# A four-layer cross-attention network on one core: where 1/sqrt is taken, which buffers a weight rounding uses, the rank of the first scans, and the place of some loads

## The chip, the cores and the metric

The kernel runs on one core of a Trainium2 chip. A core has a matrix engine (TensorE, PE in the profile; its weight loads are shown apart as PEld), VectorE (DVE), ScalarE (ACT), GpSimd (POOL), and SyncE (SP), whose only work here is to start transfers. The engines run side by side, each takes its own instructions strictly in order, and they wait for one another through semaphores. The metric is the device time of one execution in microseconds.

## What is computed

The input x has 4 batches of 512 rows and 512 columns (f32), and each batch has a context of 512 rows and 256 columns. Four layers follow; each adds a gated cross-attention part and then a gated feed-forward part (FFN) to x:

```python
x = x + tanh(g_xattn[0]) * mamba(ctx, layernorm(x))            # layer 0
x = x + tanh(g_ffn[0])   * ffn_2of4_sparse(layernorm(x))
x = x + tanh(g_xattn[1]) * attention(layernorm(x), ctx)        # layer 1
x = x + tanh(g_ffn[1])   * ffn_ternary(layernorm(x))
x = x + tanh(g_xattn[2]) * mamba(ctx, layernorm(x))            # layer 2
x = x + tanh(g_ffn[2])   * ffn_fp8_weights(layernorm(x))
x = x + tanh(g_xattn[3]) * attention_16_heads_qk_rmsnorm(layernorm(x), ctx)   # layer 3
x = x + tanh(g_ffn[3])   * ffn_1bit_weights_8bit_activations(layernorm(x))
```

The mamba parts are state-space scans: for each of 512 channels and 16 states, `state = state * exp(dt * A) + dt * u * B`, step by step over the 512 positions, and `y = sum over states of C * state`. What the scan needs (dt, u, B, C) comes from the context alone, so a scan can run well before its layer. Each layer norm, and each RMS norm of the queries and keys of layer 3, takes 1/sqrt of one number a row. In layer 2 the weights are first rounded to fp8 (e4m3) values. In layer 3's FFN activations are rounded to 8 bits a row, and the normalised hidden rows are scaled by gamma and shifted by beta.

## The kernel before

**Blocks.** x of a batch lies in four tiles of 128 x 512. `f01` (L1251) does layers 0 and 1 of a batch, `f23` (L1265) layers 2 and 3 up to the attention. They come in the order f01(0), f01(1), f23(0), f01(2), f23(1), f01(3), f23(2), f23(3), by the list `heads` (L1275). The next block's layer norm and mamba part is started inside the last matmuls of the current one (`nxt.start`, `nxt.turn`). A prologue (L1276) does the scan of layer 0, batch 0 alone. Layer 3's FFN, `l3f` (L1095), runs beside the blocks for batches 0 to 2 and alone for batch 3, as the tail (L1313).

**Side work.** Three lists of Python generators hold work to be put between the steps of the blocks: `side` (the scans, then the rounding of layer 3's weights to one bit, then `l3f`), `pres` (what comes before a scan: convolution, x_proj matmul, dt), and `prep` (the rounding of layer 2's weights to fp8, 36 half tiles). `tick(w)` (L139) gives each list credit in proportion to its rate and lets it issue steps until the credit is spent. A scan may not start before its own `pres` item is done (`waits()`). `finish(key)` issues the rest of an item at once where a block needs it. `phase[0]` is the place in `heads`, 0 to 5; 0 is f01(0).

**Order.** The lines are only recorded. A scheduler then puts each engine's instructions in order by a priority, which is the place of recording plus an offset: an instruction of lower number goes first among those that are ready. In `tick` the offset `BEHIND` is added for `prep`, and for `side` except in phase 0. The order is fixed when the kernel is built. Tiles of one tag in a pool share a fixed number of buffers, and an instruction that needs a buffer waits for those that still use it. All loads and stores named here but those of `keep` and of the scans' B and C ahead are started by SP, in order, so one that waits holds back those behind it.

**Scans.** `state` (L578) does one of 64 steps (16 states x 4 channel tiles): ACT exp into a PSUM bank `mb` (L581), POOL du x B into one of three buffers `db` (L582), DVE scan (L583), DVE times C (L584); then POOL adds into y (L602). Before it, `mamba_pre` (L472) works in four buffers of tag `mt`: it stores each u to DRAM and loads it again for the x_proj matmul (L508), one u before each of the four matmuls.

**First use of weights.** `unit` (L259) loads a raw f32 tile into one of four buffers `wr` (L264), ACT takes the high part (L256), POOL or DVE in turn the low part (L257), and the pair is stored to DRAM for later use. Later uses load the pair. This happens in f01(0) and at the start of others' first use.

**fp8 rounding.** `to_fp8` (L284) takes two buffers `wr`: one for the raw weights, one for `m`, the power of two of each element. DVE makes `m` (L290), ACT scales (L293), DVE adds and subtracts (L294, L295), and the result is stored to DRAM, from where `unit8` (L311) loads it in layer 2's FFN.

**1/sqrt.** `rsqrt` (L332) is one POOL operation, a power of -1/2 (L333), in place. `ln_stats` (L354) calls it for 1, 3 or 4 numbers a row, `kv` (L895) for 16, `q_pair` (L954) for 8, and `l3f` (L1175) for 1. DVE makes the numbers before (L363, L894, L953, L1174) and reads the result (L365, L1177), or ACT does (L899).

**Layer 3's FFN beside the blocks.** A token tile (`token`, L1129) loads x (`xl`, two buffers, L1135) and uses b1, gamma, beta and b2 spread over 128 rows (`rep`, five buffers, L1115), each loaded where it is needed. Two tokens run interleaved, the second half of one beside the first half of the next. The tail has buffers of its own, and pool `l3f` stays open while it runs.

Of the kernel before, what the change touches and what calls it, by code (L numbers as in the profile page):

```python
# [10 lines left out]
F32 = mybir.dt.float32  # L11
# [12 lines left out]
NT = S // 128  # L24
# [25 lines left out]
RATES = [0.75, 0.75, 0.75, 0.75, 0.75, 0.75, 0.75, 0.75]  # L50
RATE_FP8 = 0.15
RATE_PRE = 0.25


BEHIND = 1000
# [17 lines left out]
def tile_flamingo(ctx: ExitStack, tc: tile.TileContext, I, out):  # L73
# [65 lines left out]
    def tick(w):  # L139

        waits = lambda: side and any(k == (*side[0][0], "pre") for k, _ in pres)
        for q, r, i in ((pres, 1.0 if waits() else RATE_PRE, 0), (prep, RATE_FP8, 2), (side, rate[0], 1)):
            credit[i] += w * r
            behind = BEHIND if q is prep or q is side and phase[0] else 0
            while q and credit[i] > 0 and not (q is side and waits()):
                tc.cur_priority += behind
                try:
                    credit[i] -= next(q[0][1])
                except StopIteration:
                    q.pop(0)  # L150
                tc.cur_priority -= behind
            if not q:
                credit[i] = 0.0
# [130 lines left out]
    def to_fp8(dst, src):  # L284


        raw = T(wrp, [128, 512], F32, "wr")
        sy.dma_start(raw, src)
        m = T(wrp, [128, 512], F32, "wr")
        v.tensor_scalar(  # L290
            m.bitcast(I32), raw.bitcast(I32), 0x7F800000, 0x00400000, op0=ALU.bitwise_and, op1=ALU.bitwise_or
        )
        s.activation(raw, raw, AF.Copy, scale=2.0**-20)  # L293
        v.scalar_tensor_tensor(raw, m, 1.5 * 2.0**-6, raw, op0=ALU.max, op1=ADD)  # L294
        v.scalar_tensor_tensor(raw, m, 1.5 * 2.0**-6, raw, op0=ALU.max, op1=SUB)  # L295
        copy(dst, raw)
# [32 lines left out]
        return t  # L329


    def rsqrt(a, n):  # L332
        g.tensor_tensor(a, a, mhalf[:, :n], op=ALU.pow)  # L333

    def mm3(ps, lh, ll, rh, rl, start, stop):
        pe.matmul(ps, lh, rh, start=start, stop=False)  # L336
# [17 lines left out]
    def ln_stats(xs, small=small):  # L354
        n = len(xs)
        st = small(6 * n)
        mv = small(2 * n)
        for t in range(n):
            v.bn_stats(st[:, 6 * t : 6 * t + 6], xs[t])
# [3 lines left out]
        v.tensor_scalar(rs[:, :n], mv2[:, :, 1], EPS, None, op0=ADD)  # L363
        rsqrt(rs[:, :n], n)
        v.scalar_tensor_tensor(rs[:, n:], mv2[:, :, 0], -1.0, rs[:, :n], op0=MUL, op1=MUL)  # L365
        return rs, mv

# [104 lines left out]
    def mamba_pre(l, b, mp, pp=None):  # L472
# [24 lines left out]
            yield 2.6  # L497
        xw = M("mt")
        sy.dma_start(xw[:, :320], I[f"M{l}_xp"][0])
        xd = mbps("xd")  # L500
        for d in range(4):
            if pp:
                u = ud[d]
            else:
                u = M("mt")
                copy(u, ud[d])
            c = slice(d * 80, d * 80 + 80)
            pe.matmul(xd[:80], xw[:, c], u, start=d == 0, stop=d == 3)  # L508

        xf = M("mt")  # L510
        s.copy(xf[:80], xd[:80])
# [362 lines left out]
    def kv(b, fp):  # L874

        cu = [unit("ctxT", 2 * b + k, p=fp, tag="fc") for k in range(2)]
        for qd in range(4):
# [17 lines left out]
            rsqrt(ss[:, 16:], 16)  # L895
# [25 lines left out]
    def l3x(b, xs, xT, nxt):  # L921
        with tc.tile_pool(name=nm("r3"), bufs=2) as rp:
# [8 lines left out]
            def q_pair(p):  # L931
# [22 lines left out]
                rsqrt(ss[:, 8:], 8)  # L954
                for j in range(2):
                    qs[2 * p + j] = qn, ss[:, 8 + 4 * j : 12 + 4 * j]

# [136 lines left out]

    def l3f(b, lp, ws, ps_of=mbps, tail=None):  # L1095

        nbuf = {"rep": 5, "Y": 2, "q16": 2, "qT": 1, "yT": 4, "sq": 1, "xl": 2}
        if tail:
            nbuf = {"rep": 1, "Y": 4, "q16": 4, "qT": 2, "yT": 8, "sq": 1}

# [6 lines left out]
        kept = {}  # L1107

        def rep(n, f):

            if (n, f) in kept:
                return kept[n, f]
            tag = f"rep{n}{f}" if tail else "rep"
            r = lp.tile([128, 512], F32, tag=tag, name=nm("rep"), bufs=nbuf["rep"])
            sy.dma_start(r, I["L3_" + n][512 * f : 512 * f + 512].partition_broadcast(128))  # L1115
            if tail:
                kept[n, f] = r
            return r

        def turned(x, tag):  # L1120

# [7 lines left out]
        def token(t):  # L1129

            if tail:
                x = tail[t]
            else:
                x = L("xl", [128, 512], F32)
                sy.dma_start(x, xsc[b * NT + t])  # L1135
            rs, _ = ln_stats([x], smallL)
            yield 0.7, 1.6
            y = L("Y", [128, 2048], F32)
            z = y[:, 0:512]
            s.activation(z, x, AF.Identity, scale=rs[:, 0:1], bias=rs[:, 1:2])  # L1140
# [11 lines left out]
            for f in range(4):  # L1152
                c = slice(f * 512, f * 512 + 512)
                b1r = rep("b1", f)
                ps = ps_of("l1")
                for k in range(4):
                    pe.matmul(ps, xq[:, k * 128 : k * 128 + 128], ws["w1", k][:, f], start=k == 0, stop=k == 3)  # L1157
                v.scalar_tensor_tensor(y[:, c], ps, sc[:, 1:2], b1r, op0=MUL, op1=ADD)  # L1158
# [16 lines left out]
            rsqrt(m2[:, 3:4], 1)  # L1175
# [42 lines left out]
        gens = [token(t) for t in range(NT)]  # L1218
        if not tail:

            old = iter(())
# [78 lines left out]
    mctx.close()  # L1300
    with tc.tile_pool(name="l3f", bufs=2) as lp:
        ws3 = l3f_weights(lp)
        for b in range(2):
            side.append(((b,), l3f(b, lp, ws3)))
        rate[0] = RATES[6]
        f23(heads[6], heads[7])
        finish((1,))
        side.append(((2,), l3f(2, lp, ws3)))
        rate[0] = RATES[7]
        f23(heads[7], None)  # L1310
        finish((2,))
# [89 lines left out]
```

## Time and profile before

| | |
|---|---|
| median of three runs | 3705.31 us (3698.0 to 3706.08) |
| the profiled execution | 3685.68 us, of which the trace spans 3683.9 us |
| mean granted clock of TensorE in it | 0.928 of full speed |
| end of the prologue, by the last update of x there (L649) | 188 us |
| end of f01(0), f01(1) | 718 us, 1135 us |
| end of f23(0), f01(2), f23(1) | 1569 us, 1972 us, 2399 us |
| end of f01(3), f23(2), f23(3) | 2734 us, 3158 us, 3584 us |

The ends of blocks are taken from DVE's updates of x (L430, L437), rounded to whole microseconds. Work of neighbouring blocks overlaps at these borders. A line such as `L365 DVE SCALAR_TENSOR_TENSOR sm<-sm,sm 128x3 ... x20 | 9.6, 482 | 20.0 <-POOL sm L333 20.0` is read so: source line, engine, operation, what it writes and reads, how often, total busy time in us, mean of one in ns, idle time of the engine just before them in us, and what ended most of that idle time. In a list of waits the numbers are the total, how many, and the longest. Granted clock is a share of TensorE's full speed.

### The profile page before, as it was taken

Reading aid. Unit: us, or ns where it says so; the run is one execution under the profiler, and the core shown is the slowest. Engines: PE = TensorE matmul, PEld = TensorE weight load, DVE = VectorE, ACT = ScalarE, POOL = GpSimd, SP = SyncE. Lnnn points to the kernel's source line nnn. Section 1 sums busy time; section 2 is a strip of 40 time slices with the busy share of each in tenths; the row PEclk is TensorE's granted clock in tenths of the full one; section 3 lists DMA queues with packets and bytes.
Section 4 is the critical chain, followed back from the end, with each engine's and each line's share of the span. In section 5 each row is a group of like instructions: output and inputs, shape, how many; then the busy total and the mean of one; then the engine's idle time right before and its main releaser. Section 6 shows DMA issues by size and latency. Waiting matters only on the chain. (4 is left out here: it accounts for less than half of the span.)

```text
span 3683.9 us, 40258 instructions
## 1 busy us (share of the span) xinstructions
PE 3112.8 (84%) x12216; PEld 1979.4 (54%) x12216; DVE 2541.4 (69%) x4162; ACT 1983.4 (54%) x4405; POOL 1722.2 (47%) x1351
## 2 busy tenths in 40 slices
PE   7785875889778788899888778899999998898985
PEld 3364444565556545475565545475767554564542
DVE  7957856789688787887678878855334455454437
ACT  6455355354545667544544656543435666366644
POOL 5515856637556785744665778700101122222112
PEclk9997887999899899999999899999999999999997
DMA  8577567876876564385676543287664343554310
GB/s 272 186 264 255 182 197 257 287 250 210 272 246 208 189 187 135 108 292 189 211 243 216 169 157 106 90 296 261 227 209 163 120 135 95 166 172 122 110 42 31
DMA packets 310232, 693.10 MB, mean 188 GB/s; under 512 B 31712, under 2 KB 33120, under 8 KB 310016
## 3 DMA queue, kind: packets, MB, share of 16 engines
q1 hardware_dynamic: 256176, 589.86, 47.3%
q10 hardware_dynamic: 53840, 100.68, 9.2%
q8 instruction: 97, 1.59, 0.2%
q14 instruction: 119, 0.97, 0.1%
HBM read 525.46 MB, written 164.95 MB: 187 GB/s over the span
## 5 line engine op out<-in xcount | busy, mean ns | idle before, releaser
L581 ACT ACTIVATE mb<-dt,nA 128x512 f32<-128x512 f32 x512 | 347.1, 689 | 398.2 <-DVE db12x L584 52.0
L333 POOL TENSOR_TENSOR sm<-sm,mhalf 128x8 f32<-128x8 f32 (+4 forms) x96 | 138.8, 1446 | 483.2 <-DVE sm L363 174.1
L678 PE MATMUL gate<-xT,w 128*128 128x512 f32 x624 | 266.9, 428 | 75.4 <-ACT w L256 40.1
L985 PE MATMUL po<-pt,v 128*128 128x512 f32 x512 | 277.9, 631 | 28.3 <-ACT pt L824 22.3
L807 PE MATMUL S<-k,q 128*128 128x512 f32 x512 | 264.9, 620 | 22.2 <-ACT P L814 19.8
L814 ACT ACTIVATE P<-S,st,sm 128x512 f32<-128x512 f32 x256 | 199.9, 783 | 119.1 <-DVE st L812 117.5
L679 PE MATMUL gate<-xT,w 128*128 128x512 f32 x624 | 258.7, 415 | 1.4 <-DVE xT L257 1.4
L402 PE MATMUL acc<-w,hf 128*128 128x512 f32 x512 | 233.0, 614 | 25.6 <-DVE hf L705 14.3
L678 PE MATMUL up<-xT,w 128*128 128x512 f32 x624 | 246.7, 395 | 4.1 <-ACT w L256 4.0
L679 PE MATMUL up<-xT,w 128*128 128x512 f32 x624 | 245.6, 394 | 0.0
L808 DVE TENSOR_REDUCE st<-S 128x1 f32<-128x512 f32 x256 | 173.2, 684 | 92.9 <-PE S L807 91.2
L1003 PE MATMUL down<-wo,h 128*128 128x512 f32 x512 | 231.9, 603 | 0.7 <-DVE x L430 0.7
L333 POOL TENSOR_TENSOR sml<-sml,mhalf 128x1 f32<-128x1 f32 x32 | 18.5, 578 | 440.9 <-DVE sml L1174 229.9
L822 PE MATMUL pT<-ident,P 128*128 128x128 f32 x1024 | 168.7, 285 | 52.0 <-ACT P L814 27.3
L822 PEld LDWEIGHTS pT<-ident,P 128*128 128x128 f32 x1024 | 127.6, 146 | 136.3 <-ACT P L814 45.8
L681 PE MATMUL gate<-xT,w 128*128 128x512 f32 x432 | 181.3, 420 | 14.0 <-POOL w L257 13.8
L678 PEld LDWEIGHTS gate<-xT,w 128*128 128x128 f32 x624 | 125.0, 200 | 116.0 <-ACT w L256 41.8
L402 PEld LDWEIGHTS acc<-w,hf 128*128 128x128 f32 x512 | 99.0, 196 | 155.6 <-issue 113.3
L681 PE MATMUL up<-xT,w 128*128 128x512 f32 x432 | 169.2, 392 | 3.2 <-DVE w L257 3.2
L824 ACT COPY pt<-pT 128x512 f32<-128x512 f32 x256 | 145.9, 589 | 47.7 <-PE pT L822 46.5
L402 PE MATMUL acc<-w,h 128*128 128x512 f32 x352 | 159.7, 606 | 6.3 <-ACT fv L907 4.9
L336 PE MATMUL Q<-w,xT 128*128 128x256 f32 x512 | 156.7, 306 | 3.3 <-ACT xT L256 3.2
(288 smaller groups left out, 8971.9 us busy)
## 6 DMA issues: line engine op xcount, KB each, us to landing
bc<-dbc ACTq DMA_DIRECT2D x105, 512.0 KB, 5.7
w<-dL_g SPq DMA_DIRECT2D x81, 512.0 KB, 5.3
w<-dL_u SPq DMA_DIRECT2D x81, 512.0 KB, 4.6
w<-in_L_d_dram SPq DMA_DIRECT2D x68, 512.0 KB, 5.5
w<-dL_gu SPq DMA_DIRECT2D x48, 512.0 KB, 4.6
w<-dL_q SPq DMA_DIRECT2D x48, 512.0 KB, 5.1
rep<-in_L_b_dram SPq DMA_DIRECT2D x65, 256.0 KB, 3.9
dv<-fv ACTq DMA_DIRECT2D x64, 256.0 KB, 4.0
```

The costliest lines, as they stand in the source:

```text
L333: g.tensor_tensor(a, a, mhalf[:, :n], op=ALU.pow)
L402: pe.matmul(ps, h[:, c], w, start=first, stop=last)
L581: s.activation(ps, dt, AF.Exp, scale=nA[l][:, d * 16 + n : d * 16 + n + 1])
L678: pe.matmul(ps, wh[:, c], xT[k][:, 0], start=k == 0, stop=False)
L679: pe.matmul(ps, wh[:, c], xT[k][:, 1], start=False, stop=wl is None and k == 3)
L681: pe.matmul(ps, wl[:, c], xT[k][:, 0], start=False, stop=k == 3)
L807: pe.matmul(ps, q[:, c], k, start=True, stop=True)
L808: v.tensor_reduce(st[:, t : t + 1], ps, AX.X, ALU.max, negate=True)
L814: s.activation(p, ps, AF.Exp, scale=r, bias=m, accum_out=st[:, 8 + t : 9 + t])
L822: pe.transpose(ps[:, t * 128 : t * 128 + 128], pt[t][:, kt * 128 : kt * 128 + 128], ident)
L985: pe.matmul(po, vs[kt][:, c], u, start=kt == 0, stop=kt == 3)
L1003: pe.matmul(ps, hs[j][:, c], ws[j // 2][:, j % 2], start=j == 0, stop=j == 3)
```

## The change

- `tick` gives `side` no credit while it waits for its `pres` item, and ranks `side` behind in phase 0 too.
- `to_fp8` takes its two buffers from the tag `mt` (four, shared with `mamba_pre` and the dt weights), not from `wr`.
- `rsqrt` is done on DVE in phases 0 to 4 and the prologue, by 11 small operations: a first guess from the bits, -a/2, and three of Newton's steps of three operations each. From phase 5 on (set to 6 for the last two blocks) it stays on POOL. 62 of 128 calls move.
- `mamba_pre` loads three of the four u tiles before the first x_proj matmul, and the fourth before the last, with pauses between.
- `l3f` loads x one token ahead (three buffers `xl`) and the `rep` tiles one step ahead (seven buffers). The tokens' tiles lie in a pool of their own that is closed before the tail's pool is opened.

```diff
         for q, r, i in ((pres, 1.0 if waits() else RATE_PRE, 0), (prep, RATE_FP8, 2), (side, rate[0], 1)):
+            if q is side and waits():
+                continue
             credit[i] += w * r
-            behind = BEHIND if q is prep or q is side and phase[0] else 0
+            behind = BEHIND if q is not pres else 0
...
     def to_fp8(dst, src):
-        raw = T(wrp, [128, 512], F32, "wr")
+        raw = T(mp, [128, 512], F32, "mt")
         sy.dma_start(raw, src)
-        m = T(wrp, [128, 512], F32, "wr")
+        m = T(mp, [128, 512], F32, "mt")
...
-    def rsqrt(a, n):
-        g.tensor_tensor(a, a, mhalf[:, :n], op=ALU.pow)
+    def rsqrt(a, n, h=None, small=small):
+        if phase[0] >= SCANS:
+            g.tensor_tensor(a, a, mhalf[:, :n], op=ALU.pow)
+            return
+        w = small(2 * n if h is not None else 3 * n)
+        y, t = w[:, :n], w[:, n : 2 * n]
+        h = w[:, 2 * n :] if h is None else h
+        v.tensor_scalar(y.bitcast(I32), a.bitcast(I32), -0.5, float(0x5F3759DF), op0=MUL, op1=ADD)
+        v.tensor_scalar(h, a, -0.5, None, op0=MUL)
+        for i in range(3):
+            v.tensor_tensor(t, y, h, op=MUL)
+            v.tensor_tensor(t, t, y, op=MUL)
+            v.scalar_tensor_tensor(a if i == 2 else y, t, 1.5, y, op0=ADD, op1=MUL)
...
         sy.dma_start(xw[:, :320], I[f"M{l}_xp"][0])
+        if not pp:
+            for d in range(3):
+                u = M("mt")
+                copy(u, ud[d])
+                ud.append(u)
+            yield 2.6
         xd = mbps("xd")
         for d in range(4):
-            if pp:
-                u = ud[d]
-            else:
+            if not pp and d == 3:
                 u = M("mt")
                 copy(u, ud[d])
+                ud.append(u)
+                yield 1.3
...
-        nbuf = {"rep": 5, "Y": 2, "q16": 2, "qT": 1, "yT": 4, "sq": 1, "xl": 2}
+        nbuf = {"rep": 7, "Y": 2, "q16": 2, "qT": 1, "yT": 4, "sq": 1, "xl": 3}
...
+        def fetch(*vs):
+            if not tail:
+                for n, f in vs:
+                    ahead[n, f] = rep(n, f)
+
+        def fetch_x(t):
+            xls[t] = L("xl", [128, 512], F32)
+            sy.dma_start(xls[t], xsc[b * NT + t])
...
             rs, _ = ln_stats([x], smallL)
             yield 0.7, 1.6
+            fetch(("b1", 0))
...
+                if f < 3:
+                    fetch(("b1", f + 1))
...
+            if not tail and t + 1 < NT:
+                fetch_x(t + 1)
+            fetch(("gamma", 0), ("beta", 0))
             yield HALF, 0.0
...
                 ga, be = rep("gamma", f), rep("beta", f)
+                fetch(*((("gamma", f + 1), ("beta", f + 1)) if f < 3 else (("b2", 0),)))
...
         ws3 = l3f_weights(lp)
-        for b in range(2):
-            side.append(((b,), l3f(b, lp, ws3)))
-        rate[0] = RATES[6]
...
+        with tc.tile_pool(name="tokens", bufs=2) as lq:
+            for b in range(2):
+                side.append(((b,), l3f(b, lq, ws3)))
+            rate[0], phase[0] = RATES[6], 6
```

More of the change, by code (lines that the diff above doesn't have):

```diff
@@ L52 @@
 RATE_PRE = 0.25
+SCANS = 5
 BEHIND = 1000
@@ L363, in ln_stats @@
         v.tensor_scalar(rs[:, :n], mv2[:, :, 1], EPS, None, op0=ADD)
-        rsqrt(rs[:, :n], n)
+        rsqrt(rs[:, :n], n, small=small)
         v.scalar_tensor_tensor(rs[:, n:], mv2[:, :, 0], -1.0, rs[:, :n], op0=MUL, op1=MUL)
@@ L499, in mamba_pre @@
         sy.dma_start(xw[:, :320], I[f"M{l}_xp"][0])
+        if not pp:
[4 more added lines that the diff above has]
+            yield 2.6
         xd = mbps("xd")
         for d in range(4):
-            if pp:
-                u = ud[d]
-            else:
+            if not pp and d == 3:
                 u = M("mt")
                 copy(u, ud[d])
+                ud.append(u)
+                yield 1.3
             c = slice(d * 80, d * 80 + 80)
-            pe.matmul(xd[:80], xw[:, c], u, start=d == 0, stop=d == 3)
+            pe.matmul(xd[:80], xw[:, c], ud[d if pp else 4 + d], start=d == 0, stop=d == 3)
         xf = M("mt")
@@ L894, in kv @@
             v.tensor_scalar(ss[:, 16:], ss[:, :16], 1.0 / 128, EPS, op0=MUL, op1=ADD)
-            rsqrt(ss[:, 16:], 16)
+            rsqrt(ss[:, 16:], 16, ss[:, :16], small3)
             for kt in range(NT):
@@ L953, in q_pair @@
                 v.tensor_scalar(ss[:, 8:], ss[:, :8], 1.0 / 128, EPS, op0=MUL, op1=ADD)
-                rsqrt(ss[:, 8:], 8)
+                rsqrt(ss[:, 8:], 8, ss[:, :8], small3)
                 for j in range(2):
@@ L1105, in smallL @@
             return lp.tile([128, n], F32, tag="sm", name=nm("sml"), bufs=32 if tail else 16)
-        kept = {}
+        kept, ahead, xls = {}, {}, {}
         def rep(n, f):
@@ L1112, in rep @@
                 return kept[n, f]
+            if (n, f) in ahead:
+                return ahead.pop((n, f))
             tag = f"rep{n}{f}" if tail else "rep"
@@ L1133, in token @@
             else:
-                x = L("xl", [128, 512], F32)
-                sy.dma_start(x, xsc[b * NT + t])
+                x = xls[t]
             rs, _ = ln_stats([x], smallL)
             yield 0.7, 1.6
+            fetch(("b1", 0))
             y = L("Y", [128, 2048], F32)
@@ L1174, in token @@
             v.tensor_scalar(m2[:, 3:4], m2[:, 3:4], 1.0 / 2048, EPS, op0=MUL, op1=ADD)
-            rsqrt(m2[:, 3:4], 1)
+            rsqrt(m2[:, 3:4], 1, small=smallL)
             nms = m2[:, 4:5]
@@ L1219, in l3f @@
         if not tail:
+            fetch_x(0)
+            yield 2.0
             old = iter(())
@@ L1302, in tile_flamingo @@
         ws3 = l3f_weights(lp)
-        for b in range(2):
-            side.append(((b,), l3f(b, lp, ws3)))
-        rate[0] = RATES[6]
[L1306 to L1311, printed above, removed]
+        with tc.tile_pool(name="tokens", bufs=2) as lq:
+            for b in range(2):
+                side.append(((b,), l3f(b, lq, ws3)))
+            rate[0], phase[0] = RATES[6], 6
+            f23(heads[6], heads[7])
+            finish((1,))
+            side.append(((2,), l3f(2, lq, ws3)))
+            rate[0] = RATES[7]
+            f23(heads[7], None)
+            finish((2,))
         with psum(t=6), tc.tile_pool(name="tail", bufs=2) as tp2:
```

## The prediction

> **What bounds the kernel now.** I read the engines' totals first, then a table by stage (cut where VectorE, written DVE, finishes the four updates of x that close a block), then the waits, then the timeline at single waits.
>
> ```profile
> span 3683.9 us, 40258 instructions
> PE 3112.8 (84%) x12216; PEld 1979.4 (54%) x12216; DVE 2541.4 (69%) x4162; ACT 1983.4 (54%) x4405; POOL 1722.2 (47%) x1351
> ```
>
> The shares are means over unlike stages, so the next table decides. Its columns: stretch and length, then busy time of PE, PEld, DVE, ACT, POOL (instructions), granted clock, DMA share, GB/s.
>
> ```profile
> 188.00:718.00 530.00, 382.43 (x1292) 246.53 (x1292) 376.76 (x534) 268.79 (x582) 301.35 (x230) 0.85 0.70 238
> 718.00:1135.00 417.00, 355.54 (x1276) 236.07 (x1276) 341.83 (x494) 214.38 (x484) 234.14 (x171) 0.93 0.74 247
> 1135.00:1569.00 434.00, 364.95 (x1501) 230.76 (x1502) 361.66 (x552) 271.46 (x602) 308.31 (x243) 0.92 0.51 163
> ...
> 2399.00:2734.00 335.00, 324.39 (x1252) 224.26 (x1252) 150.22 (x277) 135.76 (x355) 24.12 (x17) 0.99 0.71 243
> ```
>
> The first, second and fourth rows are the same kind of block (batches 0, 1, 3) with about the same matmuls. Without scans beside it (last row) PE idles 11 us and the clock is 0.99; with scans it idles 61 us, and in batch 0, where weights are also split for the first time, 148 us. So PE order is the backbone, and the stages from 188 to 2399 lose time to what feeds PE. The third row is the first block of the other kind; its first 90 us (1135 to 1225, the fp8 FFN) hold 85.3 us of DVE work: there DVE is the bound.
>
> Where batch 0 loses time, the waits of PE in 188 to 718 say (in all, times, longest):
>
> ```profile
> PE gate L678 <- ACT w L256: 40.1, 4, 29.1
> PE V L336 <- ACT fw L256: 14.2, 2, 10.7
> PE gate L681 <- POOL w L257: 13.8, 8, 4.4
> ```
>
> All three wait for a freshly split weight; with the smaller rows of the same list (6.2, 4.2, 4.0, 3.5, 3.2, 1.5) it is 90.7 us. The longest, followed back:
>
> ```profile
> 604.34 0.43 SPq L288 DMA_DIRECT2D wr<-in_L_u_dram  x1
> ...
> 629.48 1.63 DVE L295 SCALAR_TENSOR_TENSOR wr<-wr,wr 128x512 f32<-128x512 f32 x1
> ...
> 631.14 0.33 SPq L265 DMA_DIRECT2D wr<-in_L_g_dram  x1
> ...
> 635.24 0.80 PE L678 MATMUL gate<-xT,w 128*128 128x512 f32 x1 [29.09 <-ACT w L256]
> ```
>
> A rounding took a wr buffer at 604.3 and gave its scratch back at 631.1; only then could the weight be loaded that PE had waited for.
>
> **The change, part by part** (minus is faster; the sum is against the profiled execution, 3685.68 us).
>
> *1. Rounding leaves the ring wr.* The 29.1 us go whole. For the other 61.6 us the ring may or may not be the cause (SP, POOL and DVE queues delay splits as well): between 0 and 61.6, and I take half, 31. **-60** (bounds -29 to -91).
>
> *2. First scans ranked behind.* In the built order DVE has done 79 scan steps instead of 103 when batch 0's first FFN ends. Priced with the groups' means, DVE's queue to that point is 364 us instead of 405. PE's other idle time in this stage is 148 - 91 = 57 us. I take **-20** (bounds 0 to -41). Next late there: normalisation and the k/v filler.
>
> *3. Newton for pow, 62 times.* POOL loses 12 of 16 wide (3.09 us each), 16 of 8 (1.66), 6 of 4 (1.02), 14 of 3 (0.86), 14 of 1 (0.55): 89 us. DVE gains 62 x 11 = 682 small operations. Such ones take about 0.155 us alone (L363 and L365 on sml below), so 1.7 us a chain. But beside scans the same lines show more:
>
> ```profile
> L365 DVE SCALAR_TENSOR_TENSOR sm<-sm,sm 128x3 f32<-128x3 f32 x20 | 9.6, 482 | 20.0 <-POOL sm L333 20.0
> L365 DVE SCALAR_TENSOR_TENSOR sm<-sm,sm 128x1 f32<-128x1 f32 x20 | 7.7, 387 | 11.6 <-POOL sm L333 11.0
> L363 DVE TENSOR_SCALAR sm<-sm 128x1 f32<-128x1 f32 x20 | 3.0, 150 | 0.4
> L365 DVE SCALAR_TENSOR_TENSOR sml<-sml,sml 128x1 f32<-128x1 f32 x16 | 2.5, 158 | 9.0 <-POOL sml L333 8.9
> ```
>
> L365 with two inputs in SBUF takes 158 ns in the quiet stages and 387 to 482 ns beside scans; singly it reached 1.25 us, about a POOL operation's length, when one was running at its start. One-column L363 stays at 150. A chain has 9 operations of L365's kind: extra between 0 and 9 x 1.07 = 9.6 us. POOL can only run ahead by the three db buffers while DVE delivers nothing, so I take about two waits, 2 us: 3.7 us a chain. From 718 to 2399, 50 chains make 185 us; DVE waits 25 us less for POOL (waits L365 <- L333, 39.3 us over the run). 160 us more on a DVE busy about 80%: its idle time takes most, and I put a fifth on the path, 32 us (bounds 0 to 160). Behind a waiting step stand scores, updates of x and scans, all of which PE or ACT wait for. Against this, POOL no longer stands at a pow with scan products queued behind it, and ACT's kn L899 no longer waits for it (81.3 us of ACT idle, little of it on PE): -12 (bounds 0 to -40). **+20**.
>
> The Trainium skill ("SBUF — State Buffer", Who interferes with whom) says that a DVE instruction with two SBUF inputs is blocked by a GpSimd instruction that reads SBUF until that one ends. The rows agree, and it speaks against this change: with every step blocked once the chain would be 11 us, and the sum over 300 us worse for DVE than I take.
>
> *4. Rounding in the ring mt* shares four buffers with the scans' preparation. In the built order 18 of 36 roundings stand before the fp8 FFN of batch 0 (all 36 before), and the rest inside it, after the seventh gate. A rounding costs DVE 0.738 + 0.893 + 1.046 = 2.68 us (L290, L294, L295): 48 us. DVE's queue in this FFN is 130 us instead of 90, where it had 85.3 busy in 90. Nothing hides it: **+42**. It is less if PE's first seven gates cover it (0), more if raw load, rounding, store and reload (each about 4 us to landing) run behind one another (+75).
>
> *5. u loaded ahead of the x_proj matmul.* L508 lost 13.8 us of PE, 8.6 to mt<-du: **-5** (bounds -14 to +10, if four held buffers block others).
>
> *6. Scans left over.* 19 steps, 36 us of DVE, pass 2399, into a stage with 185 us of idle DVE: **+3** (0 to +10). The preparation of w1/w2 stands about where it was.
>
> *7. Loads ahead in the last FFN.*
>
> ```profile
> DVE sml L359 <- DMA xl<-xsc: 47.0, 8, 10.1
> ...
> DVE Y L1158 <- DMA rep<-in_L_b_dram: 11.8, 5, 3.1
> ```
>
> DVE stands still up to 10 us for xl with score maxima queued behind: ACT's exponentials are late, then PE's transposes, at 2917 (6.7 us of PE), 3157 (7.6) and 3385 (8.9); two of 4.2 and 4.1 follow the rep waits. That is 31.5. In the built order each xl is free 13 us of DVE work or more before its use, against 3 to 10 now. **-32** (bounds -15 to -59, all of DVE's wait). The loads use the same SP queue, where L1115 already waits 118 us for POOL Y L1188; a load issued early may hold up k or v there, which is in the bound.
>
> *8. The tail.* Its tiles now lie where the tokens' tiles were. The first tail statistics wait for the last token's store; before, they started 0.7 us after the last update. After that update PE still has 16 matmuls of the last token (4.6 us at L1210's 0.29 us each), then L1213 and L1214 (1.5 us) and a store (2.4 to 4.2 us to landing for stores of 256 KB), less what overlaps the last down matmuls: **+9** (+5 to +13).
>
> Sum: -60 - 20 + 20 + 42 - 5 + 3 - 32 + 9 = **-43**: 3643 us for a profiled execution. The profiled one lies 19.6 us below the median of 3705.31; on the median the forecast is **3662 us**.
>
> **Rivals.** *B, more gain:* the ring caused all split waits (-91) and the rounding hides in waits (0): -43 - 31 - 42 = -116, 3589 us. For: DVE idles 153 us in batch 0. Against: the built order has the roundings in one block.
>
> *C, slower: Newton's steps are blocked by POOL and DVE becomes the bound between 718 and 2399.* For: L365's 1.25 us, stages with 85% DVE. All 160 us on the path instead of 32: -43 + 128 = +85; three fifths: +21; I price the middle, +50, 3755 us. It decides once more than 75 of the 160 us reach the path (32 + 43), or at the same share from about 7 us extra a chain. Against: later scans are done well ahead of their use, so delay in them costs nothing.
>
> *D, nothing:* split waits come from the queues rather than the ring, so only -29 goes, and stall moves on: about -5, 3700 us.
>
> **How the numbers follow.** A measurement tells about 0.2% (7.4 us) from no change. Forecast 0.45, B 0.15, C 0.30, D 0.10. Faster: 0.43 of the first and B, 0.58; same: 0.02 and most of D, 0.10; slower: C and 0.02, 0.32. The range 3595 to 3775 reaches nearly to B and through most of C.
>
> **What would show it.** 1: no L678 gap of tens of us near 635, and 188 to 718 shorter by about 80. 3: Newton lines at mean 0.2 to 0.4 us; over 0.7 means C. 4: PE gaps before gates in the fp8 FFN, that stretch 130 us. 7: no L359 <- xl waits. 8: 9 us between last update and first tail statistics. I am wrong if the first block keeps its length or stages 1569 to 2399 grow by over 60.

## The result, and the profile after

The changed kernel takes 3729.69 us (median of 4 runs, 3728.25 to 3737.31) where the kernel before takes 3703.17 (median of 4): a ratio of 1.0082, 95% interval 1.0067 to 1.0097. It is slower by 26.5 us; 3662 was forecast. The profiled execution took 3737.31 us against 3685.68 before, 51.6 us more, of which 17.5 come from the profiled run of before lying below that median and 7.6 from this one lying above its own.

The first lines of the page of the changed kernel:

```profile
span 3735.5 us, 40970 instructions
...
PE 3106.4 (83%) x12216; PEld 1977.1 (53%) x12216; DVE 2682.7 (72%) x4844; ACT 1983.1 (53%) x4399; POOL 1630.5 (44%) x1289
```

DVE has 682 instructions and 141 us more, POOL 62 and 92 us less, as the change says. The table by stage (columns: stretch and length, busy PE, PEld, DVE, ACT, POOL, clock, DMA share, GB/s):

```profile
192.00:673.00 481.00, 358.04 (x1259) 236.63 (x1260) 348.65 (x590) 242.03 (x534) 231.94 (x180) 0.86 0.73 238
673.00:1111.00 438.00, 359.74 (x1298) 242.59 (x1296) 363.32 (x622) 219.59 (x487) 224.95 (x171) 0.90 0.66 222
1111.00:1627.00 516.00, 379.79 (x1513) 236.22 (x1514) 414.89 (x738) 284.42 (x617) 283.47 (x224) 0.85 0.48 151
2470.00:2821.00 351.00, 334.53 (x1252) 228.81 (x1252) 188.63 (x315) 150.23 (x379) 77.52 (x57) 0.97 0.73 247
```

All borders but the one at 673 lie at the same events as before. A block ends with its own last update of x; the next block can go on only when the next batch's x has its mamba part too. Before, the block's own update was the later of the two (718), here it is the other one (first the kernel before, then the changed one):

```profile
659.54 2.73 DVE L649 SCALAR_TENSOR_TENSOR x<-xm,tgh,x 128x512 f32<-128x512 f32 x4 [2.09 <-PE xm L647]
...
717.47 0.68 DVE L437 TENSOR_TENSOR x<-acc,x 128x512 f32<-128x512 f32 x1
```

```profile
627.45 0.67 DVE L453 TENSOR_TENSOR x<-acc,x 128x512 f32<-128x512 f32 x1
...
669.95 2.73 DVE L672 SCALAR_TENSOR_TENSOR x<-xm,tgh,x 128x512 f32<-128x512 f32 x4
```

The border is put at the later one, here and in all kernels below: 673. Up to its own last update batch 0's first block takes 436 us instead of 530, up to the border 481. Against the rows of before: the first stretch 481 instead of 530, the next 438 instead of 417, the third 516 instead of 434, batch 3's first block 351 instead of 335. The third row holds the loss. The first stretch gains 49 us, though, and where 29.1 us were lost to a split weight there is another wait (waits of PE from 192 to 673: total, times, longest):

```profile
PE xm L670 <- POOL z L664: 52.5, 4, 50.3
...
PE gate L701 <- ACT w L260: 1.7, 1, 1.7
```

L670 (L647 before) turns the next batch's scan result into x. The scan was not done, and the timeline just before shows why it could not be hurried:

```profile
640.41 1.26 POOL L605 TENSOR_TENSOR db01x<-du,bc 128x512 f32<-128x512 f32 x1
641.63 1.26 POOL L625 TENSOR_TENSOR y<-y,db01x 128x512 f32<-128x512 f32 x1
641.71 1.23 DVE L606 TENSOR_TENSOR_SCAN mb<-mb,db01x 128x512 f32<-128x512 f32 x1 [1.33 <-POOL db01x L605]
```

POOL does two 1.26 us operations for each step of the scan, so the last steps run at 2.5 us each with DVE waiting for POOL. In the fp8 FFN of batch 0 (1111 to 1257, 146 us instead of 90) PE waits for rounded weights and, through the preparation of a scan, for DVE; and SP's load of raw weights for a rounding (L292) waits for a buffer `mt` that the x_proj matmul still reads:

```profile
PE gate L701 <- DMA w<-dL_gu: 25.7, 3, 10.9
PE xd L531 <- DVE db02x L607: 22.4, 1, 22.4
```

```profile
SPq L292 <- PE xd L531: 41.6, 2, 37.6
```

And this is one normalisation after it, on DVE alone (start, length, line):

```profile
1256.69 0.15 DVE L379 TENSOR_SCALAR sm<-sm 128x3 f32<-128x3 f32 x1
...
1258.10 0.14 DVE L347 TENSOR_TENSOR sm<-sm 128x3 f32<-128x3 f32 x1
1258.16 1.22 DVE L606 TENSOR_TENSOR_SCAN mb<-mb,db02x 128x512 f32<-128x512 f32 x1
1259.30 0.14 DVE L348 TENSOR_TENSOR sm<-sm 128x3 f32<-128x3 f32 x1
...
1267.45 1.23 DVE L606 TENSOR_TENSOR_SCAN mb<-mb,db02x 128x512 f32<-128x512 f32 x1 [2.53 <-POOL db02x L605]
1268.59 0.15 DVE L349 SCALAR_TENSOR_TENSOR sm<-sm 128x3 f32<-128x3 f32 x1
...
1269.33 0.67 DVE L381 SCALAR_TENSOR_TENSOR sm<-sm,sm 128x3 f32<-128x3 f32 x1
```

Most Newton steps take 0.15 us here, and the chain from L379 to L381 takes 12.6: the scheduler put scans, splits and a second chain between its dependent steps, and one of those scans waits 2.53 us for POOL. Before, the same two lines (L363, L365) stood 4.5 us apart here. PE pays it at once:

```profile
1270.92 2.32 PE L402 MATMUL lnT<-ident,t 128*128 128x128 f32 x9 [19.14 <-ACT t L391]
```

(7.38 and 3.98 us in before.) Over the 62 chains the mean from first to last Newton step is 7.0 us; from the end of pow's input to the end of pow it was 2.5. The last FFN kept its promise: no wait of DVE's first statistics (L359 before, L375 now) for xl from memory is left among the waits of DVE, where it was 47.0 us. Two small ones remain, about as before (2.5 and 1.6 us there):

```profile
DVE sml L375 <- DMA out_dram<-xl: 2.8, 1, 2.8
DVE sml L375 <- DMA rep<-in_L_b_dram: 1.8, 1, 1.8
```

### The profile page after: what moved, and what is told of

It reads as the page before. It is cut to its first block, busy times and chain, and to the rows that moved or that the text cites. A ratio compares the mean times of both kernels' runs of the same rounds, so it can differ in the third digit from the quotient of the medians.

```text
span 3735.5 us, 40970 instructions
## 1 busy us (share of the span) xinstructions
PE 3106.4 (83%) x12216; PEld 1977.1 (53%) x12216; DVE 2682.7 (72%) x4844; ACT 1983.1 (53%) x4399; POOL 1630.5 (44%) x1289
## 4 chain that ended last, share of the span: by engine, by line
PE 34%; DVE 27%; DMA 10%; POOL 9%; issue 9%; ACT 7%; SPq 1%; ACTq 0%; DVEq 0%; POOLq 0%
DVE mb L606 6%; PE S L830 4%; PE po L1008 3%; POOL y L625 3%; PE down L1026 3%; PE gate L701 2%; PE gate L702 2%; PE pT L845 2%; PE up L701 2%; PE up L702 2%; PE acc L418 2%; DMA bc<-in_L_w_dram 1%; PE l L1251 1%; DVE st L831 1%; ACT P L837 1%
## 5 line engine op out<-in xcount | busy, mean ns | idle before, releaser
L701 PE MATMUL gate<-xT,w 128*128 128x512 f32 x624 | 268.1, 430 | 66.7 <-DMA w<-dL_gu 25.7
L702 PE MATMUL up<-xT,w 128*128 128x512 f32 x624 | 245.6, 394 | 0.0
L339 POOL TENSOR_TENSOR sm<-sm,mhalf 128x8 f32<-128x8 f32 (+4 forms) x34 | 51.0, 1499 | 431.4 <-DVE sm L976 165.0
L845 PE MATMUL pT<-ident,P 128*128 128x128 f32 x1024 | 170.8, 287 | 38.9 <-ACT P L837 19.3
```

The costliest lines, as they stand in the source:

```text
L701: pe.matmul(ps, wh[:, c], xT[k][:, 0], start=k == 0, stop=False)
L702: pe.matmul(ps, wh[:, c], xT[k][:, 1], start=False, stop=wl is None and k == 3)
L845: pe.transpose(ps[:, t * 128 : t * 128 + 128], pt[t][:, kt * 128 : kt * 128 + 128], ident)
```

## The experiments

Sixteen kernels, in four groups; the kernel before ran with each group (medians 3693.42, 3693.22, 3692.54, 3693.71 us) and differences below are against it. The changed kernel ran only beside the 3703.17; where it is compared with these kernels, the ratios to the kernel before are. Stage lengths are from the profiled executions.

### One part of the change undone

**Newton undone** (a_pow).

```diff
-SCANS = 5
+SCANS = 0
```

> The changed kernel with every 1/sqrt as a pow on POOL again (SCANS = 0), all else as changed. Theory L (latency): the 11 dependent steps of a Newton chain stand in DVE's queue with other work between them, 7.0 us a chain instead of 2.5, and normalisations on PE's path pay it. Then the block after the fp8 FFN falls from 370 to about 344 us for batch 0 and from 360 to about 339 for batch 1, the wait of PE for lnT there from 19 to about 7 us, and the time from 3730 to 3655-3680. Rival P (load): the 200 us of Newton steps on DVE, blocked beside POOL, are what counts, wherever they stand: every stage between 718 and 2399 is shorter and the time falls to 3630 or below. Rival 0: the chains are hidden, 3715-3735.

3701.47 us, 1.0022 (1.0013 to 1.0032). Newton cost 0.6% here, 22 us. The stretch after the fp8 FFN fell from 369.9 to 347.7 us for batch 0 and from 360.3 to 344.0 for batch 1, as theory L said, and by the profiles these two stretches hold all of the gain. But 22 us is less than the 50 to 75 that the theory gave; batch 0's block end waits 60.0 us for the scan instead of 50.3.

**Newton as dead load** (a_dead).

```diff
+        g.tensor_tensor(a, a, mhalf[:, :n], op=ALU.pow)
         if phase[0] >= SCANS:
-            g.tensor_tensor(a, a, mhalf[:, :n], op=ALU.pow)
             return
+        a = dead[:, :n]
...
-            v.scalar_tensor_tensor(a if i == 2 else y, t, 1.5, y, op0=ADD, op1=MUL)
+            v.scalar_tensor_tensor(y, t, -1.5, y, op0=ADD, op1=MUL)
```

> The changed kernel with pow on POOL giving the 1/sqrt, and beside each of the 62 the same 11 Newton steps on DVE, on a constant, their result unused. DVE carries the same load as in the changed kernel, but nothing waits for it. Theory L: the load costs little, the time is within 15 us of the kernel with pow alone (3655-3690). Rival P: the load is what costs, within 10 us of the changed kernel (3720-3740).

3766.24, 1.0194 (1.0177 to 1.0212): 65 us above pow alone, and above the changed kernel itself. Theory L, that only the result's delay costs, falls. The rival's range was missed as well: pow stays on POOL here, and b_one1 below shows that it has a price of its own.

**Rounding back in wr** (a_wr).

```diff
-        raw = T(mp, [128, 512], F32, "mt")
+        raw = T(wrp, [128, 512], F32, "wr")
...
-        m = T(mp, [128, 512], F32, "mt")
+        m = T(wrp, [128, 512], F32, "wr")
```

> The changed kernel with the two scratch tiles of the fp8 rounding back in the ring wr. Theory R (ring shared with the scans' preparation): the roundings are spread over batch 0 again, the fp8 FFN of batch 0 falls from 146 us to 90-105, and the waits for freshly split weights come back in batch 0's first block, which gets 20-30 us longer: 3690-3715. Rival S: the burst comes from scans ranked behind, which fill DVE before it; then the fp8 FFN keeps over 125 us and the time stays above 3725.

3682.27, 0.9960 (0.9946 to 0.9975). The fp8 FFN of batch 0 is 85.8 us instead of 145.7. Batch 0's first block, up to its own last update, got longer (469.5 us against 436.0, a little more than theory R gave), but up to the border it is 235.7 + 251.8 against 227.1 + 253.5, with 28.9 us of waiting for the scan in place of 50.3. So the rounding in mt costs 1.2%, 45 us, and all but 7 us of what it gains in that block is lost again up to the border.

**Ranking undone** (a_rank).

```diff
-            if q is side and waits():
-                continue
             credit[i] += w * r
-            behind = BEHIND if q is not pres else 0
+            behind = BEHIND if q is prep or q is side and phase[0] else 0
```

> The changed kernel with the ranking of scans as before (first scans not behind, credit as before). Theory: what the ranking gains in batch 0's first FFN (47 us) is paid back where the next block needs the scan (PE's wait of 50 us for the xm operands near 664 us) and in batch 1's first FFN (246 us, 220 before). So the first FFN grows from 227 to 255-275 us, the 50 us wait falls below 15, batch 1's first FFN falls to about 225, and the time stays within 15 us of 3730. Rival (the prediction's term): ranking is a gain of 20 us that stays, time 3745-3760.

3789.74, 1.0256 (1.0240 to 1.0271): 64 us worse than the changed kernel, and both expectations missed. The first FFN stays at 230.6 us with 80 scan steps done, although scans rank as before: with the rounding in mt the second scan starts late (its first DVE step at 384 us, at 359 in b_fp8 below, at 333 in the kernel before), so ranking is not needed to make that FFN short. What the ranking does in the changed kernel shows in the fp8 FFN: without it 41 scan steps come in there (20 with it), and it takes 191.5 us. Waits of PE there:

```profile
PE gate L699 <- DMA w<-dL_gu: 56.7, 2, 45.0
PE xd L529 <- DVE db02x L605: 30.4, 1, 30.4
```

I put this down to the credit that scans no longer save up while their preparation is late; this run undoes both edits of the ranking together, so it does not show that by itself.

### One part alone on the kernel before

**Loads ahead** (b_l3f).

```diff
-        nbuf = {"rep": 5, "Y": 2, "q16": 2, "qT": 1, "yT": 4, "sq": 1, "xl": 2}
+        nbuf = {"rep": 7, "Y": 2, "q16": 2, "qT": 1, "yT": 4, "sq": 1, "xl": 3}
...
+            fetch(("b1", 0))
...
+                fetch_x(t + 1)
...
+        with tc.tile_pool(name="tokens", bufs=2) as lq:
```

> The kernel before with the last FFN's loads ahead alone (rings rep 7 and xl 3, fetch, tokens in a pool of their own, so the tail's new place too). Theory: this part is right as predicted, -32 and +9: the two stages after 2734 are 35-45 us shorter together, the tail 8 longer, all else as it was; 0.9% faster, 3655-3668 where the kernel before takes 3693. Rival: SP's queue gives it back; within 8 us of the kernel before.

3655.82, 0.9896 (0.9876 to 0.9915). The stages of the last two batches' second halves are 43.0 us shorter, the tail 8.1 longer.

**Rounding in mt** (b_fp8).

```diff
-        raw = T(wrp, [128, 512], F32, "wr")
+        raw = T(mp, [128, 512], F32, "mt")
...
-        m = T(wrp, [128, 512], F32, "wr")
+        m = T(mp, [128, 512], F32, "mt")
```

> The kernel before with the rounding's two scratch tiles in the ring mt alone. In the built order batch 0's first FFN then has 89 scan steps done instead of 103 at its end, and 17 roundings of 36 are left for the fp8 FFN instead of none. Theory (the ring mt is what is short, and preparation, scans and roundings push each other back): the first FFN 20-40 us shorter, the fp8 FFN of batch 0 40-60 us longer than its 90, and a wait for a scan at the end of batch 0's block of tens of us; 3705-3745 where the kernel before takes 3693. Rival (the prediction's two terms, -60 and +42): 3675, with batch 0's first block 60 us shorter.

3735.53, 1.0112 (1.0095 to 1.0129). The first block up to the border is 53.4 us shorter (239.3 + 237.3 against 274.2 + 255.8); the next block's FFN is 36.8 longer (256.3), the fp8 FFN 51.8 longer (141.8). There PE waits for weights that are not yet rounded:

```profile
PE gate L678 <- DMA w<-dL_gu: 44.2, 3, 28.1
```

**Newton** (b_newton).

```diff
-    def rsqrt(a, n):
-        g.tensor_tensor(a, a, mhalf[:, :n], op=ALU.pow)
+    def rsqrt(a, n, h=None, small=small):
+        if phase[0] >= SCANS:
...
+        for i in range(3):
+            v.tensor_tensor(t, y, h, op=MUL)
```

> The kernel before with Newton's steps alone for the 62 pow beside scans. The dead chains cost 65 us beside pow, and pow back in the changed kernel gained 22. Theory (a chain costs DVE and the work behind it some 1 us on the path, and pow's going gives some of it back): +15 to +40, 3708-3733 where the kernel before takes 3693, most of it in the stretches of l3x (batch 0 and 1, +15 to +25 each). Rival (rival C, DVE becomes the bound): over +50, every stage between 718 and 2399 longer. Rival (hidden): within 8 us.

3757.10, 1.0179 (1.0154 to 1.0203), more than theory said and in the rival's range. But not every stage between 718 and 2399 is longer, as the rival had it (f01(1) takes 407.6 us instead of 417.0). Batch 0 and 1 lose 32 us each in the stretch after the fp8 FFN, and the second half of batch 0's first block loses 31 more, where the first half gains 11. Waits of PE from 1224 to 1599, and in before from 1225 to 1569:

```profile
PE lnT L400 <- ACT t L389: 21.3, 4, 15.1
PE S L821 <- ACT P L828: 17.4, 3, 16.5
```

```profile
PE S L807 <- ACT P L814: 4.7, 1, 4.7
...
PE lnT L386 <- ACT t L375: 4.0, 1, 4.0
```

**Ranking** (b_rank).

```diff
+            if q is side and waits():
+                continue
             credit[i] += w * r
-            behind = BEHIND if q is prep or q is side and phase[0] else 0
+            behind = BEHIND if q is not pres else 0
```

> The kernel before with the ranking of scans alone (first scans behind; no credit saved up while a scan's preparation is awaited). In the built order 84 scan steps instead of 103 are done at the end of batch 0's first FFN. Theory: the FFN is 20-40 us shorter and the block's end waits as much longer for the next head's scan; but without saved credit scans no longer come in bursts, so 0 to -25: 3670-3693 where the kernel before takes 3693. Rival (the prediction): -20 in the first FFN with nothing late after it.

3672.91, 0.9946 (0.9931 to 0.9961). The first block up to the border is 49.2 us shorter, the FFN after it 26.2 longer. No gate waits for a split weight for more than 4.0 us; the longest wait of the block is the scan:

```profile
PE xm L649 <- POOL z L643: 36.5, 3, 34.5
```

So ranking alone takes away the wait that the rounding's move was for, and pays with the same wait for the scan.

### What Newton's price is made of, and what adds up

**Dead load on the kernel before** (b_dead): pow kept, the 11 steps of a_dead beside it.

```diff
         g.tensor_tensor(a, a, mhalf[:, :n], op=ALU.pow)
+        if phase[0] >= SCANS:
+            return
+        a = dead[:, :n]
...
+            v.scalar_tensor_tensor(y, t, -1.5, y, op0=ADD, op1=MUL)
```

> The kernel before, pow kept on POOL, and beside each of the 62 pow the 11 Newton steps on DVE on a constant, their result unused: DVE gets the load, nothing waits for the result, POOL keeps its pow. Newton alone cost 64 us here. Theory L (the result's delay, 7.0 us a chain instead of 2.5, is what costs): below +25. Theory P (DVE's load, some 140 us of busy time, costs by itself, 65 us in the changed kernel): +45 to +75, spread over the blocks of batch 0 to 2 rather than in the two stretches after the fp8 FFN alone.

3753.47, 1.0172 (1.0149 to 1.0194). Load alone costs 61 us; theory P holds. It is spread: +19 in batch 0's first block, +5.5 and +19.3 in the stretches after the fp8 FFNs, +10 in batch 2's first FFN.

**No 1/sqrt** (b_one1; one instruction writes ones, so this part is left out).

```diff
-        g.tensor_tensor(a, a, mhalf[:, :n], op=ALU.pow)
+        v.tensor_scalar(a, a, 0.0, 1.0, op0=MUL, op1=ADD)      # beside scans
```

> The kernel before with the 62 pow left out: one DVE instruction writes ones in their place, so the 1/sqrt is not computed and only the work around it is timed. It shows what pow on POOL costs at all, the most that any replacement could gain. The prediction's term was -12 for POOL's relief (bounds 0 to -40). Theory (POOL's relief and the shorter normalisation are worth something, as Newton in place of pow cost less than Newton's load beside pow in the changed kernel): -15 to -45, 3648-3678. Rival (nothing waits for POOL there): within 8 us of 3693.

3638.73, 0.9855 (0.9837 to 0.9874): pow on POOL costs 54 us, more than the theory's 45. A replacement gains only if it costs less than these 54 us, and Newton's steps cost 118 (54 + 64).

**The two parts that gained** (b_l3f_rank): the diffs of b_rank and b_l3f together.

> The kernel before with the two parts that gained, the ranking of scans and the last FFN's loads ahead, and neither Newton's steps nor the rounding in mt nor u ahead. They lie in different stages, so the gains should add, -20 - 38: 3635 (3625-3648), faster than both kernels. Rival (they share a cause): no better than 3655.

3634.34, 0.9844 (0.9822 to 0.9866): they add, and this beats both kernels.

**The same with u ahead** (a_wr_pow).

```diff
+            for d in range(3):
+                u = M("mt")
+                copy(u, ud[d])
+                ud.append(u)
+            yield 2.6
```

> The same with u loaded ahead of the x_proj matmul as well, that is the changed kernel without Newton's steps and without the rounding in mt. The prediction gave u ahead -5 (bounds -14 to +10). Theory (the PE waits for u go, but three more buffers of four are held in the ring mt at once, and 490 scan steps instead of 512 are done at the end of batch 1's second block): -8 to +12 against the kernel with the two parts alone. Rival: the parts' sum in the changed kernel, 30 us over the kernel before, is 20 us less than that of Newton (+64), rounding (+42), ranking (-20) and loads (-38) measured singly, and u ahead is the missing -20.

3645.75, 0.9878 (0.9853 to 0.9902): u ahead costs 11 us here. Only 490 scan steps of 512 are done when batch 1 ends (512 without it), and the rest make batch 3's first FFN 199.4 us instead of 178.3. The rival, that u ahead is the missing gain, falls: the singles now sum to +60 (64 + 42 - 20 - 37 + 11) against +26.5, so the parts overlap by some 33 us.

**A shorter chain** (b_newt2, best_newt2): two steps, 7 or 5 instructions.

```diff
+        v.tensor_scalar(y.bitcast(I32), a.bitcast(I32), -0.5, float(0x5F3759DF), op0=MUL, op1=ADD)
+        for i in range(2):
+            if n == 1:
+                v.scalar_tensor_tensor(t, y, a, y, op0=MUL, op1=MUL)
+            else:
+                v.tensor_tensor(t, y, a, op=MUL)
+                v.tensor_tensor(t, t, y, op=MUL)
+            v.scalar_tensor_tensor(a if i else y, t, -12.0 if i else -3.0, y, op0=ADD, op1=MUL)
```

> The kernel before with a shorter chain in place of the 62 pow: two of Newton's steps instead of three, the factors folded into the operation before, 7 instructions (5 for one column) instead of 11, 406 in all instead of 682. One step less leaves out the last bits of 1/sqrt. Measured so far, against the kernel before: no 1/sqrt at all -54, three steps +64, so three steps cost 118 us. Theory (the cost goes with DVE's instructions): 118 x 406/682 = 70, that is +16, 3709 (3698-3720). Rival (a fixed price for each chain, whatever its length: handing over, being queued behind scans): over +40.

> The kernel with ranked scans and loads ahead (3634, -58), with the same shorter chain in place of pow. In the ranked surroundings three steps cost 36 us more than pow (3682 against 3646). Theory (cost by instructions): 36 + 54 = 90 for three steps, 54 for the short chain, which is pow's own price: 3634 (3622-3648). Rival (fixed price): over 3650. Below 3622 pow's price would be larger here than in the kernel before.

3729.90, 1.0100 (1.0085 to 1.0115), and 3665.11, 0.9923 (0.9901 to 0.9946). The first lies between theory and rival, the second in the rival's range (over 3650). Against no 1/sqrt the short chain costs 90 us (36 + 54), not 70. By DVE's busy time on the page it fits: the kernel without 1/sqrt has 2554.6 us, this 2650.1, three steps 2682.8, so 90 us for 95.5 and 118 for 128.2, 0.94 and 0.92 us of time for each us of DVE. That was seen afterwards and not tested by another run. In the ranked kernel the short chain loses 30 us to pow, where three steps lost 36: pow on POOL stays the cheaper one, and there a fixed price for each chain is not excluded.

**Two rings of two** (b_own22, best_own).

```diff
-    wrp = mctx.enter_context(tc.tile_pool(name="wr", bufs=4))
+    wrp = mctx.enter_context(tc.tile_pool(name="wr", bufs=2))
+    w8p = mctx.enter_context(tc.tile_pool(name="w8", bufs=2))
...
-        raw = T(wrp, [128, 512], F32, "wr")
+        raw = T(w8p, [128, 512], F32, "w8")
```

> The kernel before with rounding's scratch in a ring of its own of two buffers, and the ring wr cut to two for the splits (there is no room for more). In the built order scans, preparation and roundings stand nearly as before (101 scan steps at the end of the first FFN, 31 roundings of 36 before the fp8 FFN). Theory (a rounding in wr holds up the splits): the 29 us wait of a gate for a split weight near 635 us goes; splits have two buffers at least to themselves; batch 0's first block 20 to 60 us shorter, the fp8 FFN up to 12 longer: 3650-3690 where the kernel before takes 3693. Rival (the queues, or the count of buffers, hold up the splits): the waits stay, 3690-3730.

> The kernel with ranked scans and loads ahead (3634), with the same two rings of two. There the wait at the end of batch 0's block is for a scan (34.5 us) and no longer for a split weight. Theory: little is left to gain from the ring, 3625-3645. Rival (the ring still costs as in the kernel before): as much gain as in the kernel before, 3600-3615.

3705.24, 1.0037 (1.0023 to 1.0051), and 3676.29, 0.9959 (0.9945 to 0.9972), 41 us worse than the ranked kernel, outside both ranges. In b_own22 the 29.1 us wait is gone and batch 0's first block is 14.5 us shorter:

```profile
PE gate L681 <- POOL w L257: 16.5, 8, 4.4
...
PE gate L678 <- ACT w L256: 11.8, 4, 5.4
```

The theory named that wait rightly, but the time is in the rival's range: with two buffers the prologue, where weights are split, takes 203.4 us instead of 188.2, and the first FFN of batch 1, where none is split but roundings run, 233.9 instead of 219.6. So the rounding in wr held that split up, and the two rings of two cost more than that; which of the two rings costs the second loss isn't shown. Larger rings weren't tried.

## Why the prediction was wrong, by its steps

The sum was -43; the profile went +51.6 and the medians +26.5. "Newton alone +64" and the like are differences of medians. Measured singly, the move of the rounding (steps 1 and 4) came out at +42 instead of -18 and Newton (step 3) at +64 instead of +20: these are the steps that failed.

1. *Rounding leaves wr, -60.* The waits went as said: the longest of a gate for a split weight is 3.1 us in the changed kernel (POOL w), and this part alone brings the block's own last update 71 us nearer to the prologue's end. The step that failed is what is late next: the next batch's x waits for its scan, and that comes 474 us after the prologue in the kernel before, 477 with this part, 481 with the ranking and 481 in the changed kernel. So 53 us are left at the border, and 13 at the end of f01(1).
2. *First scans ranked behind, -20.* Alone -20.3, but that the number fits is luck: -49 in the block (bound -41), +26 in the next FFN. "Next late there: normalisation and the k/v filler" was wrong; it is the scan itself, whose last steps run at POOL's 2.5 us. **Steps 1 and 2 remove the same stall**: as long as the scan comes no earlier, at most the 56 us between 662 and 718 can be gained in that block; each alone takes about 50 of them, together 49, where I added 80. Of these 49 the changed kernel has 28 left at the end of f01(1).
3. *Newton, +20.* Alone +64, in the changed kernel +22; why it is less there isn't shown. The chain was sized well: 682 instructions took 203 us, mean 0.298 us (3.7 us a chain assumed, 3.3 measured). The failed term is "a fifth on the path": 61 us of b_dead's 138 more on DVE, 0.44, with nobody waiting for the result. My reading, which no run shows by itself: where DVE is 80% busy in the mean, what it feeds waits at its busy moments. The second failed term is the relief, -12 (bounds 0 to -40): no pow at all gives -54. A third was missing: a chain of dependent instructions is stretched by what the scheduler puts between them; that cost 54 + 64 - 61 = 57 us if the three add, which no run tested. On that reckoning Newton gave back pow's 54 by its own delay, and its load was the net.
4. *Rounding in mt, +42.* In its stage +55.7 (b_fp8 +51.8); the stretch is 146 us, 130 forecast, with 17 roundings inside where 18 were expected. The term was too small because DVE's queue is not all of it: DVE is busy for 110.7 of the 146 us (118.2 of 142 in b_fp8), and the rest goes to what the forecast had only in its upper bound, loads and roundings that wait for one another: PE 25.7 us for rounded weights, a rounding's load up to 37.6 us for a buffer `mt`. The first FFN of batch 1 is 26.3 us longer in the changed kernel, but not because of mt: it takes 245.9 us there and 245.6 in a_wr.
5. *u ahead, -5.* +11. Just beyond the bound of +10, which named held buffers as the reason; the 37.6 us wait for a buffer `mt` above fits that: a_pow has it too (34.7 us), b_fp8, without u ahead, has not.
6. *Scans left over, +3.* Batch 3's first FFN grew by 14.3 us, beyond the bound of 10. Beside the ranking, u ahead leaves them over: 490 steps done with it, 512 without, +21 us. It takes both: in a_rank (u ahead, no ranking) and in b_rank (ranking, no u ahead) all 512 are done.
7. *Loads ahead, -32.* -44 in these stages (-20 and -24), -43.0 alone.
8. *Tail, +9.* +8.4.

Rival C, slower by Newton's load on DVE, had the right sign and part of the mechanism: DVE's load does cost by itself. But its sign for that, Newton lines at a mean over 0.7 us, did not appear (0.298), and it does not carry the changed kernel by itself, since the rounding in mt costs twice as much there (+45 against Newton's +22). Of the signs named beforehand, "the first block keeps its length" didn't happen; the stages 1569 to 2399 (1627 to 2470 now) grew by 13 us, not 60: the loss lay in 718 to 1569, of which I had named only the fp8 FFN.

The Trainium skill ("SBUF — State Buffer", Who interferes with whom) says that GpSimd reading SBUF blocks a DVE instruction with two SBUF inputs until it ends. The trace agrees for the one instruction: of the steps at L347 to L349 in the changed kernel, 159 started with a POOL instruction under way and took 0.685 us in the mean, 399 started without and took 0.160. Of the 159, the 116 that took over 0.2 us ended 0.02 us (median) after that POOL instruction. For the sum the measurement decides: two or three steps of nine meet a POOL instruction, not all, and the +300 us for the case that all do did not come.

What stays open: why the ranked kernel lets Newton cost 36 us (3682 against 3646) and the kernel before 64; how much of the 57 us is the order in DVE's queue, as a chain kept in one piece wasn't run; and where the 33 us by which the parts overlap lie.

## What to carry to other kernels

Two edits that remove the same stall are priced together, and the sum must name what the stage waits for once it is gone: here a scan that POOL paces at 2.5 us a step. Moving small work to an engine that is 70% busy cost about half of its busy time here even with nobody waiting for it (61 of 138 us), and a chain of small dependent instructions in a shared in-order queue is priced with what is put between them (7.0 us in the mean, of which 3.3 are its own steps; 12.6 us at one place on the path). A ring that was lent to one more user delayed the others here: look at who prepares what in it before moving a user there.

## What the runs showed of the hardware

Waiting went with a lower granted clock here. In the fp8 FFN of batch 0, with the same 300 matmuls:

```profile
1111.00:1257.00 146.00, 85.73 (x300) 62.31 (x300) 110.66 (x158) 51.34 (x82) 60.20 (x45) 0.77 0.51 159
```

```profile
1111.00:1196.00 85.00, 73.39 (x300) 55.90 (x300) 72.46 (x99) 40.69 (x66) 53.52 (x41) 0.95 0.59 185
```

The first row is the changed kernel, the second b_rank: PE is busy 59% of the one stretch and 86% of the other, and at clock 0.77 it needs 12.3 us more for the same work than at 0.95. Over all runs the mean clock goes from 0.931 (3629.5 us span) to 0.907 (3786.2).

A DVE instruction with one input can be held up by POOL as well, when it is wider than one column. Of the 62 that write ones in b_one1 (0.47 us in the mean), 29 of 3 to 16 columns started with a POOL instruction under way and took 0.82 us, 19 of these widths started without and took 0.16, and the 14 of one column took 0.14 either way. The prediction had read only the one-column L363, at 150 ns.
